# Cross-attention on one core: the first batch in another order, and T4 summed by accumulating DMAs

## The chip, the cores and the metric

The kernel runs on one core of a Trainium2 chip. The metric is the device time of one execution in microseconds; lower is better. Before the change the median of three runs is 695.43 us (695.27 to 696.22). Times inside the profile are microseconds from the first instruction of the profiled execution. PE is TensorE, DVE VectorE, ACT ScalarE, POOL GpSimd, SP SyncE; L12 is line 12 of the kernel.

## The reference

For each of 8 batches, with 512 channels and 1024 positions, all in float32:

```python
q = jnp.einsum('bcn,dc->bnd', x1, Wq) + bq              # d = 64
k = jnp.einsum('bcn,dc->bdn', x2, Wk) + bk[:, None]
v = jnp.einsum('bcn,dc->bdn', x2, Wv) + bv[:, None]
attn = jax.nn.softmax(jnp.einsum('bnd,bdm->bnm', q, k), axis=2)
return jnp.einsum('bcm,bnm->bcn', v, attn) + x1
```

## The kernel before

*Two products per batch.* The kernel never forms v. It first multiplies x2 by the attention weights (the y stage), then the result by Wv (the o stage), and adds bv and x1 at the end. Both products are cut into two by two blocks and done with Winograd's form of Strassen's algorithm: seven block products in place of eight, for sums of blocks that are formed beforehand. In the y stage the left blocks are `a["11"]` to `a["22"]` (x2, transposed by the host), the right ones `t["11"]` to `t["22"]`, which are the exponentials: `e[h]` holds the scores of one half h of the queries against all keys, 128 x 2 x 4 x 512, where the second axis is the half g of the keys and the third a tile i of 128 keys. So `t["11"]` and `t["21"]` are the two halves of `e[0]`, `t["12"]` and `t["22"]` those of `e[1]`.

The sums of the left blocks are S1 to S4 (`sum_a`, `left_sums`, L100), those of the right ones T1 to T4 (`sum_e`, `right_sums`, L258). Each is one operation of VectorE on 128 x 1024 elements, or for the T sums two, one for each pair of key tiles. `MULT` (L292) says which pair a product takes: product 1 takes 11 and 11, 2 takes 12 and 21, 6 takes S2 and T2, 7 takes S3 and T3, 5 takes S1 and T1, 3 takes S4 and 22, and 4 takes 22 and T4.

*A second level.* Products 3 and 4 of the y stage (and product 2 from batch 1 on) are cut once more in the same way: `inner_left` and `inner_right` form the inner sums (tiles aI and eI) on VectorE, `inner_product` (L362) multiplies them. `inner_right(s, 4, T4)` reads T4, and is its only reader. Within an inner product TensorE takes the inner products in the order 1, 7, 6, 2, 5, 4, 3: the first needs no sums, the second needs the inner S3 and T3, and T3 is the third of the four sums that `inner_right` forms.

*Softmax.* The scores of a tile are made by TensorE (`scores`) and copied to `e` by ScalarE. VectorE folds the tiles of a half into a maximum (`fold`, "max"), GpSimd takes it over the partitions (`highest`, a partition_all_reduce), VectorE subtracts it (`lower`, or `first_exponentials` for half 0 of the first batch), ScalarE takes the exponential. The denominators are sums of the same tiles: folds on VectorE (`sums`) or, for half 0 of the batches from 1 on, DMAs that add a tile onto another (`add_tile`); then `total` reduces them over the partitions on GpSimd and starts a small DMA into `few`; `shares` takes the reciprocal on VectorE and spreads it again by two DMAs (`row`, then `den`), the second waiting for the first.

*Order.* The kernel runs under a manual schedule: each engine executes its instructions in the order in which the code issues them, and waits by semaphores. `head` opens batch 0, `head_second` finishes its half 1, and `period` runs one batch and, woven in, the scores of the next. GpSimd's queue holds the column reductions and all accumulating and small DMAs; SP's holds the loads and stores. An instruction that waits holds back all that is behind it on its engine.

What matters of the order of VectorE in `period`: for batches from 1 on, T1 and T2 (`sum_e`), the sums of half 1, the evictions of product 2, T4 (`sum_t4`), S4, T3, then `inner_right` of product 4 (eI4), `inner_left` of product 3 (aI3), the maxima of the next batch's half 0, the four subtractions of that maximum, then `inner_right` of product 3 (eI3). In batch 0 the maxima come ahead of eI4 and the subtractions behind eI3. On GpSimd, for batches from 2 on: the shares of half 0 (`row`, `den`), the second denominator with its `few`, then the column maximum of the next batch. In batch 1 both denominators come first and the shares of half 0 behind them.

In `head`, VectorE forms S1 and S2 after it has handed the maximum of half 0 to GpSimd and before it subtracts the reduced maximum; TensorE makes three pairs of scores of half 1 (a pair is one tile of keys in both halves) ahead of product 1, and the fourth in `head_second`.

## Time and profile before

| what | value |
|---|---|
| median of the runs | 695.43 us (695.27 to 696.22) |
| the profiled execution's own time | 694.83 us |
| its span, first to last instruction | 693.0 us |
| TensorE busy | 685.8 us, 99% |
| VectorE busy | 604.5 us, 87% |
| ScalarE busy | 255.2 us, 37% |
| GpSimd busy | 186.9 us, 27% |
| queue of GpSimd's DMAs | 29.96 MB, 25.7% of 16 engines |
| granted TensorE clock | 1.000 |

A row of a timeline gives start, duration, engine, line, operation, the tile written and those read, the shapes, and how many instructions were merged; in brackets stands the idle time of the engine before it and what ended it. Names of tiles lose their numbers there: eT is any of T1, T2, T4, and eI the inner sums of any product. A DMA's row on GpSimd is its issue; when its data has landed stands in the list of issues, as a time from the issue. TensorE's matmuls are pipelined and their ends are modelled. Spans on GpSimd are rough.

### The profile page before, as it was taken

What the parts mean: (1) busy time and instruction counts of PE and PEld (TensorE: products, weight loads), DVE (VectorE), ACT (ScalarE), POOL (GpSimd) and SP (SyncE); (2) the same over time, 40 slices, a digit from 0 to 9 for tenths busy, and PEclk for the clock granted to TensorE, in tenths of its full rate; (3) what the DMA queues carried; (4) which work ended last, traced back from release to release, by engine and by line L of the source; (5) the groups of instructions that cost most, each with busy time, mean ns of one, the idle gap of its engine ahead of it and who ended that gap; (6) DMA issues with size and microseconds to landing.
All of it is one profiled execution on the core that took longest, in us unless ns stands there. A gap on an engine that the chain in (4) does not pass through costs nothing.

```text
span 693.0 us, 6395 instructions
## 1 busy us (share of the span) xinstructions
PE 685.8 (99%) x2188; PEld 353.4 (51%) x2188; DVE 604.5 (87%) x756; ACT 255.2 (37%) x402; POOL 186.9 (27%) x135
## 2 busy tenths in 40 slices
PE   8999999999999999999999999999999999999997
PEld 5333554535545355454654546454554545545563
DVE  1999999988999878998789987999689998999685
ACT  2733353145242543235432344413444235241120
POOL 0123113512322125222162222522223222423000
PEclk9999999999999999999999999999999999999999
DMA  9676256953567463865639457284742743369103
GB/s 307 254 233 226 58 183 129 260 157 76 183 128 210 149 116 142 166 183 151 107 138 191 157 166 181 67 190 140 183 78 55 172 136 60 77 115 251 31 1 121
DMA packets 42992, 102.72 MB, mean 148 GB/s; under 512 B 4688, under 2 KB 6992, under 8 KB 42960
## 3 DMA queue, kind: packets, MB, share of 16 engines
q1 hardware_dynamic: 25856, 70.13, 29.1%
q0 software_dynamic: 15696, 29.96, 25.7%
q10 hardware_dynamic: 1408, 2.23, 1.0%
q8 instruction: 17, 0.28, 0.2%
q14 instruction: 15, 0.12, 0.0%
HBM read 72.62 MB, written 16.81 MB: 129 GB/s over the span
## 4 chain that ended last, share of the span: by engine, by line
PE 95%; DMA 2%; ACT 1%; DVE 1%; SPq 1%; issue 0%; DVEq 0%
PE ps_ya L312 24%; PE ps_oa L312 16%; PE ps_i L362 14%; PE ps_oc L312 12%; PE ps_yc L312 9%; PE ps_s L190 6%; PE ps_k L148 4%; PE ps_q L148 4%; PE ps_yc L362 3%; PE ps_ya L362 3%; DMA a<-in_x2T_dram 1%; DMA x_head<-in_x_dram 1%; PE ps_sc L190 1%; PE ps_sa L190 1%; DVE aS L109 0%; ACT e L199 0%
## 5 line engine op out<-in xcount | busy, mean ns | idle before, releaser
L312 PE MATMUL ps_ya<-eT,aS 128*128 128x512 f32 x256 | 113.1, 596 | 0.0
L323 ACT COPY uy<-ps_ya 128x512 f32<-128x512 f32 x48 | 28.0, 587 | 163.8 <-PE ps_ya L312 158.0
L225 POOL PARTITION_ALL_REDUCE den<-sum x16 | 69.4, 4337 | 44.0 <-DVE sum L214 39.0
L248 DVE TENSOR_TENSOR e<-e,top 128x1024 f32<-128x1024 f32 x60 | 69.8, 1215 | 10.9 <-POOL top L220 10.9
L312 PEld LDWEIGHTS ps_ya<-eT,aS 128*128 128x128 f32 x256 | 48.0, 190 | 60.8 <-issue 59.7
L220 POOL PARTITION_ALL_REDUCE top<-max x16 | 31.3, 1957 | 162.4 <-DVE few L233 74.9
L252 ACT ACTIVATE e<-e 128x1024 f32<-128x1024 f32 x60 | 61.3, 1054 | 21.6 <-DVE e L248 20.1
L362 PE MATMUL ps_i<-eI,aI 128*128 128x256 f32 x276 | 66.0, 380 | 0.3 <-ACT e L199 0.3
L312 PE MATMUL ps_yc<-e,a 128*128 128x512 f32 x144 | 63.4, 593 | 0.0
L312 PE MATMUL ps_oa<-yT,w_S 128*128 128x512 f32 x128 | 57.6, 593 | 0.0
L312 PE MATMUL ps_oc<-y,w 128*128 128x512 f32 x128 | 57.5, 592 | 0.0
L312 PE MATMUL ps_ya<-e,a 128*128 128x512 f32 x128 | 56.3, 593 | 0.3 <-ACT e L243 0.3
L362 PEld LDWEIGHTS ps_i<-eI,aI 128*128 128x128 f32 x276 | 51.9, 190 | 8.2 <-ACT e L199 0.7
L199 ACT COPY e<-ps_s 128x1024 f32<-128x1024 f32 x46 | 45.7, 1028 | 19.1 <-PE ps_s L190 17.9
L323 ACT COPY uo<-ps_oa 128x512 f32<-128x512 f32 x48 | 27.9, 584 | 64.3 <-PE ps_oa L312 58.1
L190 PE MATMUL ps_s<-q,k 64*128 64x512 f32 x188 | 47.3, 608 | 0.8 <-ACT q L553 0.8
L261 DVE TENSOR_TENSOR eT<-e,eT 128x1024 f32<-128x1024 f32 x32 | 47.0, 1489 | 0.5
L312 PEld LDWEIGHTS ps_yc<-e,a 128*128 128x128 f32 x144 | 27.3, 190 | 34.8 <-issue 33.6
L521 POOL DMA_DIRECT2D sum<-e x21 | 25.7, 1224 | 69.5 <-DMA sum<-e 54.8
L371 ACT COPY d<-ps_i 128x256 f32<-128x256 f32 x64 | 22.3, 375 | 57.9 <-PE ps_i L362 57.9
L517 POOL DMA_DIRECT2D uo<-in_x_dram x21 | 25.0, 1191 | 68.9 <-DVE uo L514 63.1
L312 PEld LDWEIGHTS ps_ya<-e,a 128*128 128x128 f32 x128 | 24.3, 190 | 31.3 <-issue 29.6
(119 smaller groups left out, 1098.7 us busy)
## 6 DMA issues: line engine op xcount, KB each, us to landing
x_in_x_dram<-in_x_dram SPq DMA_DIRECT2D x60, 512.0 KB, 6.0
a<-in_x2T_dram SPq DMA_DIRECT2D x32, 512.0 KB, 7.0
sum<-e POOLq DMA_DIRECT2D x21, 512.0 KB, 5.1
uo<-in_x_dram POOLq DMA_DIRECT2D x21, 512.0 KB, 6.5
out_dram<-uo SPq DMA_DIRECT2D x21, 512.0 KB, 4.1
den<-row POOLq DMA_DIRECT2D x16, 256.0 KB, 3.5
r<-in_x_dram POOLq DMA_DIRECT2D x7, 512.0 KB, 5.9
out_dram<-r SPq DMA_DIRECT2D x7, 512.0 KB, 8.3
```

Of the source, the lines that this page charges most:

```text
L148: nc.tensor.matmul(ps[r, :], w_sb[:, c, :], s.x[:, c, ts(h, H)], start=(c == 0), stop=(c == CT - 1),)
L190: nc.tensor.matmul(ps[g], s.k[r, ts(i, P)], s.q[r, ts(h, H)], start=True, stop=True)
L199: nc.scalar.copy(e[:, :, i, :], whole)
L220: nc.gpsimd.partition_all_reduce(s.top[h], s.mx[h][:, 0, :], P, ReduceOp.max)
L225: nc.gpsimd.partition_all_reduce(s.den[h], s.mx[h][:, 0, :], P, ReduceOp.add)
L248: nc.vector.tensor_tensor(e, e, top, ALU.subtract)
L252: nc.scalar.activation(e, e, AF.Exp)
L261: nc.vector.tensor_tensor(t[k], t[x], t[y], ALU.subtract)
L312: nc.tensor.matmul(ps[:, n], left[ka][:, k, ts(j, P)], right[kb][:, k, n], start=opens and k == 0, stop=i in (2, 3, 4) and k == n_k - 1, s ...
L323: nc.scalar.copy(s.tmp[i][:, j, :], ps)
L362: nc.tensor.matmul(ps, s.inner[i][ka][:, k, :], s.inner[i, "t"][kb][:, k, :], start=opens and k == 0, stop=z in (2, 3, 4) and k == MH // 2 ...
L521: nc.gpsimd.dma_start(s.mx[h], s.e[h][:, :, i, :], accum_op=ALU.add)
```

## The change

Six things, of which the first concerns only the form of the second:

1. S2 becomes 11 - S1 where it was S1 - 11, and T2 becomes T1 - 22 where it was 22 - T1. S4 and T4 add S2 and T2 where they subtracted them. Both factors of product 6 change sign, so it stays; S4 and T4 stay as they were. The same holds for the inner sums and for the o stage.
2. `sum_t4` no longer uses VectorE: ScalarE copies the block 21 into T4 in two halves, and two DMAs on GpSimd's queue add the halves of T2 to it. `sum_t4` stands in `period` and is called once for every batch.
3. In `head`, S1 and S2 are formed behind the subtractions of half 0.
4. The third pair of scores of half 1 is made behind product 1, in `head_second`, and its copies with it.
5. The fold of tile 1 into the sum of half 0 comes after the fold of tile 1 into the maximum of half 1.
6. The folds of tiles 2 and 3 into the sum of half 0 come in `period` behind T1 and T2, for batch 0 alone.

```diff
@@ left_sums, and the same in LEFT
-                "S2": ("S1", "11", ALU.subtract),
+                "S2": ("11", "S1", ALU.subtract),
...
-                "S4": ("12", "S2", ALU.subtract),
+                "S4": ("12", "S2", ALU.add),
@@ right_sums, and the same in RIGHT
-        x, y = {"T1": ("12", "11"), "T2": ("22", "T1"), "T3": ("22", "12"), "T4": ("21", "T2")}[k]
-        nc.vector.tensor_tensor(t[k], t[x], t[y], ALU.subtract)
+        x, y = {"T1": ("12", "11"), "T2": ("T1", "22"), "T3": ("22", "12"), "T4": ("21", "T2")}[k]
+        nc.vector.tensor_tensor(t[k], t[x], t[y], ALU.add if k == "T4" else ALU.subtract)
@@ sum_t4
-        s.t["T4"] = sb.tile([P, MH, H], F32, tag="eT4", name=f"eT4_{s.b}")
-        sum_e(s, "T4")
+        s.t["T4"] = t4 = sb.tile([P, MH, H], F32, tag="eT4", name=f"eT4_{s.b}")
+        for i in (0, 2):
+            nc.scalar.copy(t4[:, i : i + 2, :], s.t["21"][:, i : i + 2, :])
+        for i in (0, 2):
+            nc.gpsimd.dma_start(t4[:, i : i + 2, :], s.t["T2"][:, i : i + 2, :], accum_op=ALU.add)
@@ head
         highest(s, 0, halves=False)
-        sum_a(s, "S1", "S2")
         more_queries(*tiles[1:])
         load_x(states[1], x1)
-        copies = [scores(s, 1, 0), scores(s, 1, 1), scores(s, 1, 2, "c")]
+        copies = [scores(s, 1, i) for i in range(2)]
         for g in range(2):
             for i in range(MH):
                 first_exponentials(s, g, i)
         for copy in copies:
             copy()
+        sum_a(s, "S1", "S2")
+        fold(s, 1, 1, "max", ALU.max)
         fold(s, 0, 1, "sum", ALU.add)
-        fold(s, 0, 2, "sum", ALU.add)
-        fold(s, 1, 1, "max", ALU.max)
-        fold(s, 0, 3, "sum", ALU.add)
@@ head_second
-        scores(s, 1, 3)()
+        copies = [scores(s, 1, 2, "c"), scores(s, 1, 3)]
+        for copy in copies:
+            copy()
@@ period
         sum_e(s, "T1", "T2")
+        if s.b == 0:
+            for i in range(2, MH):
+                fold(s, 0, i, "sum", ALU.add)
         if s.b < 2:
             total(s, 0)
```

More of the change, by code (lines that the diff above doesn't have):

```diff
@@ L326 @@
         ("S1", "21", "22", ALU.add),
-        ("S2", "S1", "11", ALU.subtract),
+        ("S2", "11", "S1", ALU.subtract),
         ("S3", "11", "21", ALU.subtract),
-        ("S4", "12", "S2", ALU.subtract),
+        ("S4", "12", "S2", ALU.add),
     )
@@ L332 @@
         ("T1", "12", "11", ALU.subtract),
-        ("T2", "22", "T1", ALU.subtract),
+        ("T2", "T1", "22", ALU.subtract),
         ("T3", "22", "12", ALU.subtract),
-        ("T4", "21", "T2", ALU.subtract),
+        ("T4", "21", "T2", ALU.add),
     )
```

## The prediction

> **What bounds the kernel now.** I read the page's busy shares and its chain first, then the list of what TensorE waited for, then the timelines of VectorE, GpSimd and TensorE around the products that read T4, and last the landing times of accumulating DMAs.

> ```profile
> PE 685.8 (99%) x2188; PEld 353.4 (51%) x2188; DVE 604.5 (87%) x756; ACT 255.2 (37%) x402; POOL 186.9 (27%) x135
> PE 95%; DMA 2%; ACT 1%; DVE 1%; SPq 1%; issue 0%; DVEq 0%
> ```
> ```profile
> PE ps_warm L598 <- DVE warm L595: 1.0, 1, 1.0
> PE ps_q L549 <- DMA x_head<-in_x_dram: 1.0, 1, 1.0
> PE ps_s L190 <- ACT q L553: 0.8, 1, 0.8
> PE ps_ya L312 <- ACT e L243: 0.3, 1, 0.3
> PE ps_i L362 <- ACT e L199: 0.3, 1, 0.3
> ```
> TensorE is the bound, and its waits sum to 3.4 us; after 25 us it waits once, 0.29 us at 590 us. So work taken from VectorE gains next to nothing, and whatever makes TensorE wait is paid in full. The question is how much slack each step has, and T4 has the least to spare: here is batch 1, from VectorE, GpSimd and TensorE in turn.

> ```profile
> 138.15 2.33 DVE L261 TENSOR_TENSOR eT<-e,eT 128x1024 f32<-128x1024 f32 x2
> 143.80 0.68 DVE L355 TENSOR_TENSOR eI<-eT 128x512 f32<-128x512 f32 x1
> 154.30 4.63 DVE L248 TENSOR_TENSOR e<-e,top 128x1024 f32<-128x1024 f32 x4 [1.82 <-POOL top L220]
> 160.18 0.69 DVE L355 TENSOR_TENSOR eI<-e 128x512 f32<-128x512 f32 x1
> ```
> ```profile
> 137.76 0.59 POOL L227 DMA_DIRECT2D few<-den  x1 [0.30 <-POOL den L225]
> 141.00 0.54 POOL L237 DMA_DIRECT2D den<-row  x1 [1.93 <-DMA row<-few]
> 152.49 1.78 POOL L220 PARTITION_ALL_REDUCE top<-max  x1 [10.95 <-DVE few L233]
> ```
> ```profile
> 160.27 1.03 PE L362 MATMUL ps_i<-e,aS 128*128 128x256 f32 x4
> 161.14 1.89 PE L362 MATMUL ps_i<-eI,aI 128*128 128x256 f32 x8
> ```
> L261 at 138.15 is T4. L355 at 143.80 opens eI4, the right sums of product 4, and reads T4. Behind it VectorE does, without a gap, aI3, the maxima of the next batch, their column maximum on GpSimd (the one idle of 1.82), four subtractions, and eI3, whose third sum T3 runs 160.18 to 160.87. TensorE reads that T3 at 161.14: slack 0.27 us.

> **The change, part by part.** The definition of T4 is shared, so all eight batches get the copies and the DMAs, not the first alone.

> *Signs.* S2, S4, T2, T4 keep their shapes and counts: nothing.

> *T4 on its engines.* VectorE loses two operations of 2.33 to 2.34 us together per batch (4.64 beside a reduction). ScalarE gains two copies of 128x1024, 1.03 each by L529, 2.1 per batch; in batches 1 to 6 they fall into the 4.79 us it idles before the copies of product 6, in batch 7 into 5.83, in batch 0 between 48.4 and 51.3: hidden, with 0.8 us left in batch 0. GpSimd gains two DMA issues of about 1.2 us. In batches 1 to 7 they stand between the denominators and the column maximum, where GpSimd idles 7.0 to 13.4 us; in batch 0 they stand ahead of the second denominator, after the first one's issue. SP's queue is not touched.

> *When T4 lands.* The profile has no T4 DMA; the nearest rows are the 21 sums that add an SBUF tile to an SBUF tile, also 512 KB, and one place where two accumulating DMAs are issued back to back:

> ```profile
> sum<-e POOLq DMA_DIRECT2D x21, 512.0 KB, 5.1
> ```
> ```profile
> 108.74 1.19 POOL L517 DMA_DIRECT2D uo<-in_x_dram  x1 [9.04 <-DVE uo L514]
> 109.49 1.66 POOL L521 DMA_DIRECT2D sum<-e  x1
> ```
> ```profile
> uo<-in_x_dram POOLq DMA_DIRECT2D x1, 512.0 KB, 5.7
> sum<-e POOLq DMA_DIRECT2D x1, 512.0 KB, 7.4
> ```
> The first landed 5.7 us after its issue, the second 7.4 after its own: at 116.9, 2.5 us behind the first and 8.15 us after the first issue. T4's two start from a source like the sums (5.1), so I take 7.9 us from the first issue to both landed. Ends: 7.45 (fastest sum 5.0, plus 2.45) and 9.5 (the pair issued at 117.22 and 117.94, queued behind a third, was in at 126.7). I go by the rows, because they are accumulating DMAs on the same queue.

> [...]

> *What VectorE then waits for.* eI4 needs both halves. Without T4, VectorE is there 2.3 us sooner than before, and the DMAs are later than that in every batch from 1 on. Delay of eI4 = landing minus its old start; all up to eI3 follows it, the 1.82 us wait for the maximum too, as that reduction stands behind eI4. Stall of TensorE = old end of T3 in eI3 + delay + 0.1 (the exponential at 24.29 took 0.60, TensorE began at 24.97) minus the time at which TensorE read it. From the timelines (us):

> | batch | first T4 issue | both in | old eI4 start | delay | old T3 end | TensorE reads | stall |
> |---|---|---|---|---|---|---|---|
> | 1 | 141.57 | 149.9 | 143.80 | 6.1 | 160.87 | 161.14 | 5.9 |
> | 2 | 221.62 | 229.5 | 225.31 | 4.2 | 242.36 | 245.60 | 1.1 |
> | 3 | 305.05 | 313.0 | 309.73 | 3.2 | 326.79 | 330.06 | 0.1 |
> | 4 | 389.76 | 397.7 | 394.44 | 3.2 | 411.49 | 414.52 | 0.3 |
> | 5 | 474.30 | 482.2 | 477.99 | 4.2 | 495.05 | 498.98 | 0.4 |
> | 6 | 558.82 | 566.7 | 562.50 | 4.2 | 579.56 | 579.86 | 4.0 |
> | 7 | 639.70 | 647.6 | 642.25 | 5.4 | 648.37 | 653.88 | 0 |

> The issue is 0.57 after GpSimd's last earlier DMA (few of half 1; in batch 1 den<-row at 141.00, whose 256 KB, in at 144.5, I give 0.4 us in front of T4). Batch 6 has little slack because TensorE has no queries to project there; batch 1 because its aI4 comes later and GpSimd does the first shares late. Sum: 11.8 us. Each batch's GpSimd chain is started by TensorE's results, so a stall in one batch shifts the next as a whole and is not given back. What comes behind eI3 on VectorE is covered: it idled 2.8 to 4.2 us before L431 in batches 1 to 5, and in batch 6, where only 1.4, L431 waits for the stalled TensorE. The exponentials behind the subtractions end late on ScalarE too: its copy of the first inner bank then comes about 0.4 us after TensorE restarts, inside the 0.86 us of the product in between.

> *Batch 0.* T4 is issued near 56 and in at about 64.5; eI4 stands at 68.79: hidden, by 4 us. *The opening:*

> ```profile
> 20.45 1.22 DVE L109 TENSOR_TENSOR aS<-a,a 128x1024 f32<-128x1024 f32 x1
> 21.71 1.94 DVE L109 TENSOR_TENSOR aS<-aS,a 128x1024 f32<-128x1024 f32 x1
> 23.57 4.89 DVE L242 TENSOR_TENSOR e<-e,top 128x512 f32<-128x512 f32 x8
> ```
> S1, S2 leave this place; the reduction that runs beside them (20.63, 2.68 us) takes 1.77 where VectorE only waits (318.43). Then the subtractions begin at 22.44 instead of 23.57, and product 1 at 23.84 instead of 24.97: minus 1.13. But the third pair of scores, 0.86 us that TensorE did in this gap, now stands behind product 1: net minus 0.27. If the reduction stays at 2.68, minus 0.2 plus 0.86, so plus 0.66. S1 and S2 go behind the subtractions, 27.3 to 29.7, where VectorE next waits for a copy that ends near 29.9. The maximum of half 1 is then asked for at 36.4 (36.62), and T2's second half is done near 48.75, 0.3 us before product 6 reads it. The two late sums (2.4 us) fill the place of T4 (2.35), so eI3 of batch 0 stays near 76.13 to 76.5 against TensorE at 76.3: plus 0 to 0.2, taken as 0.1. Opening and batch 0: minus 0.2.

> *Sum.* 11.8 - 0.2 = plus 11.6 on the profiled execution: span 693.0 to 704.6, its time 694.83 to 706.4. The median of the runs, 695.43, stands 0.6 above that execution: 707.0. At the ends of the landing the stalls come to 9.7 us (7.45) and 22.9 us (9.5), with the opening 704.9 and 719.

> **The rivals.** *Not slower: T4 lands before VectorE asks.* Decisive are batches 1 and 6: slack 0.2 us, so T4 would have to be in 2.4 us (by 144.0) and 3.9 us (by 562.7) after its first issue. Then only the opening counts: 695.2. For it: VectorE loses 2.3 us of work per batch. Against it: it then only waits sooner, and of the 21 sums none landed under 5.0.

> *Slower by less: the halves move side by side.* If the second half lands 6.8 us or less after the first issue (1.7 behind the first), batches 2 to 5 are free, and 1 and 6 give 4.8 and 2.9: 703.0; if both are in after 5.1, 3.1 and 1.2, so 699.5. Against it: the 2.5 us between the two landings at 114.4 and 116.9.

> *Slower by more: the queue is fuller.* At 9.5 us each batch from 2 to 5 pays 1.7 to 2.7 and batch 7 some 1.5: 718. For it: the sums range up to 7.4. Against it: in batch 3 the loads issued at 299.16 are the last on the other queue until 315.47, so T4 moves nearly alone.

> **How the numbers follow.** Forecast 0.76; side by side 0.10; fuller queue 0.10; not slower 0.04. The forecast holds 704.9 to about 711 (landing up to 8.5). Taking in most of the second and a good part of the third gives 702 to 714. A measurement of this kernel tells about 0.2% (1.4 us) from no change; beyond that on the fast side nothing in the rows could carry it: the opening has 1.1 us to give. Faster 0.01, same 0.03, slower 0.96.

> **What would show it.** TensorE's waits list inner products (L366) on VectorE's eI: about 5 to 6 us at batch 1 and 4 at batch 6, the longest. VectorE idles 4 to 8 us before eI4 (L359), released by the DMA eT<-eT. T4's pair lands 7.5 to 8.5 us after its first issue. Product 1 opens near 23.9. It is wrong if eI4 waits for nothing, if T4 lands in under 6 us, or if the longest new wait stands elsewhere, such as at batch 0's T2.

## The result and the profile after

The changed kernel takes 718.11 us (median of 5 runs, 715.97 to 726.01) against 695.43 us: ratio 1.0337, 95% interval 1.0309 to 1.0365. The profiled execution took 716.75 us with a span of 715.0, so the span grew by 22.0 us where the prediction had 11.6. The direction, the wait and its places came as predicted; the sum had no term for TensorE's clock, priced the stalls too short, and came to about half. The range ended at 714 and did not hold the time.

Busy shares, the clock row and the chain from the page of the changed kernel:

```profile
PE 692.5 (97%) x2188; PEld 356.4 (50%) x2188; DVE 585.3 (82%) x740; ACT 272.2 (38%) x418; POOL 200.7 (28%) x151
...
PEclk9999999998999999999999999999999998999999
...
PE 21%; DMA 2%; DVE 2%; issue 1%; ACT 1%; POOL 1%; DVEq 0%; ACTq 0%; POOLq 0%
```

VectorE does 19.2 us less than before, ScalarE 17.0 and GpSimd 13.8 more. TensorE runs the same 2188 matmuls, but its busy time is 6.7 us higher, and two digits of the clock row are an 8. That is the first sign of a loss that is not a wait. The chain here is followed back only to 506 us and its shares are not those of the whole span.

What TensorE waited for (total, times, longest):

```profile
PE ps_i L366 <- ACT sum L533: 15.6, 5, 6.4
PE ps_warm L602 <- DVE warm L599: 1.0, 1, 1.0
PE ps_s L190 <- ACT q L557: 0.8, 1, 0.8
PE ps_q L553 <- DMA x_head<-in_x_dram: 0.7, 1, 0.7
```

One new wait, at inner product 7 of product 3 as predicted. The row names ScalarE's first copy of the next sum, because that ended last, 0.05 us ahead; what inner product 7 waits for in the program is VectorE's third sum in eI3. In batch 1 that sum ends at 167.90 and TensorE goes on at 168.05. The same 0.15 us lie between the two in batch 0 of the run with T4 on VectorE below, where ScalarE makes no such copy and the row names VectorE. Batch 1 from VectorE, GpSimd and TensorE, then the stalls of the other batches:

```profile
150.82 0.69 DVE L359 TENSOR_TENSOR eI<-eT 128x512 f32<-128x512 f32 x1 [8.85 <-DMA eT<-eT]
...
161.34 4.63 DVE L248 TENSOR_TENSOR e<-e,top 128x1024 f32<-128x1024 f32 x4 [1.83 <-POOL top L220]
...
167.22 0.68 DVE L359 TENSOR_TENSOR eI<-e 128x512 f32<-128x512 f32 x1
```
```profile
141.64 0.54 POOL L237 DMA_DIRECT2D den<-row  x1 [2.21 <-DMA row<-few]
142.16 1.79 POOL L276 DMA_DIRECT2D eT<-eT  x2
```
```profile
160.62 1.03 PE L366 MATMUL ps_i<-e,aS 128*128 128x256 f32 x4
168.05 3.75 PE L366 MATMUL ps_i<-eI,aI 128*128 128x256 f32 x8 [6.40 <-ACT sum L533]
...
257.34 1.97 PE L366 MATMUL ps_i<-eI,aI 128*128 128x256 f32 x8 [1.84 <-ACT sum L533]
342.97 1.97 PE L366 MATMUL ps_i<-eI,aI 128*128 128x256 f32 x8 [0.93 <-ACT sum L533]
513.42 1.97 PE L366 MATMUL ps_i<-eI,aI 128*128 128x256 f32 x8 [1.29 <-ACT sum L533]
599.67 3.75 PE L366 MATMUL ps_i<-eI,aI 128*128 128x256 f32 x8 [5.13 <-ACT sum L533]
```

T4 is asked for at 142.16, and at 150.82 VectorE, idle for 8.85 us, starts eI4. Here and below a pair of DMAs counts as in, or landed, when VectorE starts on it; the record of the landing itself lies some 0.1 us earlier (150.69). The reader should also compare the second number of the five rows: the same eight matmuls, inner products 7 and 6, take 1.97 us in three batches and 3.75 us behind the two long stalls. The view by stretches, cut into four pieces of 3.41 us, shows why (after the length: busy time and count of TensorE, its weight loads, VectorE, ScalarE, GpSimd; then the granted clock, the DMA share and GB/s):

```profile
163.36:166.78 3.42, 0.00 (x0) 0.00 (x0) 3.39 (x5) 3.18 (x4) 0.56 (x1) 1.00 0.27 77
166.78:170.19 3.41, 2.14 (x5) 1.81 (x6) 2.93 (x5) 1.55 (x4) 1.23 (x1) 0.50 0.04 7
170.19:173.60 3.41, 3.41 (x9) 2.69 (x9) 0.00 (x0) 0.69 (x2) 0.00 (x1) 0.50 0.86 147
173.60:177.02 3.42, 3.42 (x16) 2.44 (x17) 1.71 (x3) 0.65 (x2) 1.21 (x1) 1.00 0.54 93
```

After a stretch in which TensorE did nothing, its clock is 0.50 for two such stretches, 6.83 us, and TensorE does 9 matmuls in the time of 16 or so. Two halved stretches come once more, from 596.86 us, there behind a stretch in which TensorE idled for 2.32 of 3.41 us.

With this the 22.0 us can be added up. "Stall" is the start of inner product 7, less the start of inner product 1 of the same product, less the 0.87 us between them without a wait; "half clock" is half of the time that TensorE worked at 0.50; "lateness" is the start of product 3 after the change less that before, which shows the term of the batch above.

| batch | lateness at product 3 | stall | half clock |
|---|---|---|---|
| 1 | 0.35 | 6.56 | 2.8 |
| 2 | 9.73 | 2.00 | 0 |
| 3 | 11.81 | 1.09 | 0 |
| 4 | 12.98 | 0 | 0 |
| 5 | 12.99 | 1.44 | 0 |
| 6 | 14.51 | 5.29 | 2.0 |
| end | 22.0 | | |

0.35 + 16.4 + 4.8 = 21.5; the other 0.5 us is spread.

### The profile page after: what moved, and what is told of

The parts are those of the page before. It is cut to its first block, busy times and chain, and to the rows that moved or that the text cites. A ratio compares the mean times of both kernels' runs of the same rounds, so it can differ in the third digit from the quotient of the medians.

```text
span 715.0 us, 6445 instructions
## 1 busy us (share of the span) xinstructions
PE 692.5 (97%) x2188; PEld 356.4 (50%) x2188; DVE 585.3 (82%) x740; ACT 272.2 (38%) x418; POOL 200.7 (28%) x151
## 5 line engine op out<-in xcount | busy, mean ns | idle before, releaser
L366 PE MATMUL ps_i<-eI,aI 128*128 128x256 f32 x276 | 70.1, 396 | 15.9 <-ACT sum L533 15.6
L225 POOL PARTITION_ALL_REDUCE den<-sum x16 | 68.9, 4308 | 42.5 <-DVE sum L214 42.3
L220 POOL PARTITION_ALL_REDUCE top<-max x16 | 30.6, 1915 | 173.0 <-DVE few L233 88.4
L248 DVE TENSOR_TENSOR e<-e,top 128x1024 f32<-128x1024 f32 x60 | 69.8, 1217 | 11.0 <-POOL top L220 11.0
L366 PEld LDWEIGHTS ps_i<-eI,aI 128*128 128x128 f32 x276 | 53.9, 199 | 26.3 <-ACT sum L533 17.5
L199 ACT COPY e<-ps_s 128x1024 f32<-128x1024 f32 x46 | 45.7, 1028 | 18.9 <-PE ps_s L190 18.4
L327 ACT COPY uo<-ps_oa 128x512 f32<-128x512 f32 x48 | 28.0, 585 | 64.5 <-PE ps_oa L316 57.2
L359 DVE TENSOR_TENSOR eI<-eT 128x512 f32<-128x512 f32 x16 | 11.0, 688 | 49.1 <-DMA eT<-eT 49.1
L190 PE MATMUL ps_s<-q,k 64*128 64x512 f32 x188 | 47.2, 607 | 0.8 <-ACT q L557 0.8
L316 PEld LDWEIGHTS ps_yc<-e,a 128*128 128x128 f32 x144 | 27.3, 190 | 34.8 <-issue 33.6
L521 POOL DMA_DIRECT2D uo<-in_x_dram x21 | 25.1, 1195 | 67.6 <-DVE uo L518 67.6
L210 DVE TENSOR_TENSOR max<-max,e 128x1024 f32<-128x1024 f32 x30 | 36.8, 1226 | 4.4 <-ACT e L197 1.0
## 6 DMA issues: line engine op xcount, KB each, us to landing
x_in_x_dram<-in_x_dram SPq DMA_DIRECT2D x60, 512.0 KB, 6.8
a<-in_x2T_dram SPq DMA_DIRECT2D x32, 512.0 KB, 6.5
sum<-e POOLq DMA_DIRECT2D x21, 512.0 KB, 5.3
uo<-in_x_dram POOLq DMA_DIRECT2D x21, 512.0 KB, 6.4
out_dram<-uo SPq DMA_DIRECT2D x21, 512.0 KB, 4.7
eT<-eT POOLq DMA_DIRECT2D x16, 512.0 KB, 6.1
r<-in_x_dram POOLq DMA_DIRECT2D x7, 512.0 KB, 7.3
```

Source lines behind the costliest of these rows:

```text
L190: nc.tensor.matmul(ps[g], s.k[r, ts(i, P)], s.q[r, ts(h, H)], start=True, stop=True)
L199: nc.scalar.copy(e[:, :, i, :], whole)
L210: nc.vector.tensor_tensor(f, e[:, :, 0, :] if i == 1 else f, e[:, :, i, :], op)
L220: nc.gpsimd.partition_all_reduce(s.top[h], s.mx[h][:, 0, :], P, ReduceOp.max)
L225: nc.gpsimd.partition_all_reduce(s.den[h], s.mx[h][:, 0, :], P, ReduceOp.add)
L248: nc.vector.tensor_tensor(e, e, top, ALU.subtract)
```

## The experiments

Theory A: the whole loss is TensorE waiting because VectorE waits for T4's DMAs ahead of eI4, plus the halved clock behind the longest of these stalls. Rivals: B, the new opening has a part in it; C, the copies and the added DMA traffic slow other things; D, the halved clock has another cause than idle time of TensorE. Two more come later, on what sets the landing of an early T4: F, the loads that move at the same time, and G, the reduction that GpSimd runs beside it. Where lines of T4's code are added or left out, line numbers differ by a few.

**T4 on VectorE, opening as changed.**

```diff
-            nc.scalar.copy(t4[:, i : i + 2, :], s.t["21"][:, i : i + 2, :])
-        for i in (0, 2):
-            nc.gpsimd.dma_start(t4[...], s.t["T2"][...], accum_op=ALU.add)
+        sum_e(s, "T4")
```

> The changed kernel with T4 computed on VectorE again in all batches (no copies, no accumulating DMAs); signs and opening stay as changed. Theory A (the whole loss is TensorE waiting because VectorE waits for T4's DMAs, plus the halved clock behind the two longest of these stalls): inner product 7 waits in no batch, granted clock 1.000, time 695.0 to 696.3. In the changed kernel's trace TensorE reaches product 3 of batch 1 0.35 us later than before (160.62 against 160.27), so near 695.8. Theory B (the new opening has a part in the loss): 698 or more.

Measured: 697.86 us, 1.0037 (1.0024 to 1.0049), clock 0.999 to 1.000. Most of the loss is gone, but not all: 2.4 us stay, where theory A had at most 0.9; theory B's sign, 698 or more, is missed by 0.1. The trace puts most of them in batch 0, 2.2 us in two waits of TensorE:

```profile
57.70 1.13 PE L190 MATMUL ps_s<-q,k 64*128 64x512 f32 x4 [0.58 <-ACT e L199]
78.83 1.96 PE L362 MATMUL ps_i<-eI,aI 128*128 128x256 f32 x8 [1.62 <-DVE eI L355]
```

The two sums that the change moved to batch 0 (2.4 us on VectorE) have no room there unless T4 leaves VectorE in that batch, just as the prediction's batch 0 step had it. So the opening is not free by itself; it is paid by batch 0's T4.

**T4 by copies and DMAs in batch 0 alone.**

```diff
+        if s.b > 0:
+            sum_e(s, "T4")
+            return
         for i in (0, 2):
             nc.scalar.copy(...)
```

> The changed kernel with T4 by copies and DMAs in batch 0 alone, on VectorE in the others: signs and opening as changed. The kernel with T4 on VectorE everywhere (697.9) lost 1.6 us at eI3 of batch 0, behind the two sums that came there; with T4 off VectorE in that batch this stall goes. Theory A: no wait of TensorE above 0.3 us after 25 us, clock 1.000, 694.9 to 695.7, the same as with eI4 behind eI3 (695.1). Theory B (the opening costs something by itself): 697 or more.

Measured: 695.58 us, 1.0003 (0.9994 to 1.0012). After 25 us TensorE waits nowhere for more than 0.3 us. With the run above it shows that batch 0's DMAs are worth 2.3 us to the new opening (697.86 to 695.58), and that opening and batch 0 together come to no change. Theory B falls: what costs 22 us is T4 in batches 1 to 7.

**T4 alone, opening as before.** The kernel before, with the signs and the new `sum_t4`.

> The kernel before with the signs and the copies and accumulating DMAs for T4 alone; the opening stays as before. Theory A: the same stalls of inner product 7 as in the changed kernel (about 6.5, 2, 1, 0, 1.5, 5 us in batches 1 to 6), granted clock 0.98 to 0.99, 715 to 720. Theory B: below 712, by as much as the opening costs.

Measured: 717.3 us, 1.0309 (1.0265 to 1.0353), runs 713.01 to 721.11. Stalls in the profiled run:

```profile
168.70 3.75 PE L366 MATMUL ps_i<-eI,aI 128*128 128x256 f32 x8 [7.62 <-ACT sum L533]
258.32 1.97 PE L366 MATMUL ps_i<-eI,aI 128*128 128x256 f32 x8 [2.02 <-ACT sum L533]
344.25 1.97 PE L366 MATMUL ps_i<-eI,aI 128*128 128x256 f32 x8 [1.23 <-ACT sum L533]
514.15 1.97 PE L366 MATMUL ps_i<-eI,aI 128*128 128x256 f32 x8 [0.73 <-ACT sum L533]
600.66 3.75 PE L366 MATMUL ps_i<-eI,aI 128*128 128x256 f32 x8 [5.39 <-ACT sum L533]
```

Same places, same sizes within 1.2 us, the same loss. This is theory A again.

**eI4 behind eI3.** Copies, DMAs and traffic stay; only the order on VectorE differs.

```diff
         if s.b:
-            inner_right(s, 4, s.t["T4"], "eT2")
             inner_left(s, 3, s.a["S4"], "aI3")
...
         if s.b:
             inner_right(s, 3, s.t["22"], "eT1")
+            inner_right(s, 4, s.t["T4"], "eT2")
```

> The changed kernel with the right sums of product 4 (eI4, the reader of T4) moved behind the right sums of product 3 (eI3) in batches 1 to 7. Copies, accumulating DMAs and their traffic all stay; only nothing of eI3 is queued behind the wait for T4 any more. Theory A: no stall of inner product 7, clock 1.000, 694.8 to 696.3; eI4 waits for no DMA, as T4 lands some 8 us before VectorE gets to it. Theory C (the copies on ScalarE and the 8 MB more on the GpSimd queue slow other things by themselves): 700 or more, with waits at other places.

Measured: 695.13 us, 0.9995 (0.9986 to 1.0003). What TensorE waited for in this kernel is short:

```profile
PE ps_warm L602 <- DVE warm L599: 1.0, 1, 1.0
PE ps_s L190 <- ACT q L557: 0.8, 1, 0.8
PE ps_q L553 <- DMA x_head<-in_x_dram: 0.6, 1, 0.6
PE ps_i L366 <- ACT e L199: 0.3, 1, 0.3
```

All 16 copies and 16 DMAs are there and cost nothing: theory C falls. The 23 us are not the price of the DMAs but of what was queued behind their wait on VectorE. This version beats the changed kernel by 23 us and cannot be told from the kernel before: VectorE has some 14 us less to do (590.9 busy, before 604.5), and since TensorE is busy 99% of the span in both, that buys nothing.

**T4 on VectorE in batches 1 and 6 alone.** `if s.b in (1, 6): sum_e(s, "T4"); return` ahead of the copies.

> The changed kernel with T4 on VectorE in batches 1 and 6 alone, the two with the long stalls. Theory A: the stalls of batches 2, 3 and 5 stay at 2.0, 1.1 and 1.4 us, none of them halves the clock (1.000), and the time is 695.8 plus 4.5: 699 to 701.5. Theory D (the halved clock comes from something other than the length of the stall): clock below 1.000 still, 702 or more.

Measured: 702.56 us (700.63 to 705.86), 1.0107 (1.0081 to 1.0132), 1 us over the expectation's end. The remaining stalls were 1.93, 2.10 and 1.23 us, as expected in batches 2 and 5 and 1 us longer in batch 3; and the clock, which theory A had at 1.000, fell once, behind that stall:

```profile
334.46:337.88 3.42, 1.32 (x7) 0.87 (x6) 3.35 (x7) 2.62 (x4) 0.69 (x1) 1.00 0.19 62
337.88:341.29 3.41, 3.41 (x10) 2.65 (x9) 2.17 (x5) 0.74 (x2) 0.54 (x1) 0.50 0.76 131
341.29:344.70 3.41, 3.41 (x17) 2.58 (x17) 1.56 (x3) 0.65 (x2) 1.20 (x1) 1.00 0.20 35
```

A stall of only 2.10 us, over at 336.94, was followed by 3.41 us at 0.50 from 337.88. So a stall as long as those of batches 1 and 6 (6.40 and 5.13 us) is not needed: theory A in the form written down, with a halved clock behind the longest stalls alone, is too simple. Both signs that the expectation gave for theory D came, a clock below 1.000 and 702 us or more. What is left to test is whether idle time of TensorE is the cause at all. In this profiled run TensorE also came to the scores behind product 6 of batch 0 1.6 us later than in the changed kernel (56.55 against 54.99), which may be part of the 3.0 us by which it is longer than the next of the four.

**VectorE made late without any DMA.** The kernel before, the first sum of eI4 repeated.

```diff
-            nc.vector.tensor_tensor(v[k], v[x], v[y], op)
+            for _ in range(REPEAT[s.b] if i == 4 and z == 0 else 1):
+                nc.vector.tensor_tensor(v[k], v[x], v[y], op)
+    REPEAT = (1, 4, 11, 12, 13, 15, 5, 1)
```

> The kernel before (T4 on VectorE, no new DMA), with the first sum of eI4 done over again 3, 10, 11, 12, 14 and 4 times more in batches 1 to 6, at 0.6 us each: VectorE comes late to eI3 by 1.8, 6.1, 6.7, 7.3, 8.5 and 2.4 us. Theory A (lateness of VectorE before eI3 is all there is to it): less the slack of each batch (0.1, 3.1, 3.1, 2.9, 3.8, 0.15 with 0.15 us for the signal) inner product 7 stalls about 1.7, 3.0, 3.6, 4.4, 4.7 and 2.3 us, 19.7 in all, and behind the stalls over about 3 us the clock is halved for one or two windows of 3.4 us, each costing up to 1.7 to 3.4 us: 695.4 + 19.7 + 6 to 13 = 721 to 728. Theory D (the halving belongs to the DMAs): the same stalls, clock 1.000, about 715.

Measured: 735.92 us, 1.0592 (1.0572 to 1.0612). A repeat took 0.72 us (four in 2.86), not 0.6, so VectorE was late by 2.2 to 10 us and the waits came to 26.4 us instead of 19.7. The time lies beyond theory A's 721 to 728 and far from theory D's 715:

```profile
163.50 1.97 PE L365 MATMUL ps_i<-eI,aI 128*128 128x256 f32 x8 [2.29 <-ACT sum L532]
252.20 3.75 PE L365 MATMUL ps_i<-eI,aI 128*128 128x256 f32 x8 [4.01 <-ACT sum L532]
343.88 3.75 PE L365 MATMUL ps_i<-eI,aI 128*128 128x256 f32 x8 [4.35 <-ACT sum L532]
437.02 3.75 PE L365 MATMUL ps_i<-eI,aI 128*128 128x256 f32 x8 [5.58 <-ACT sum L532]
531.45 3.75 PE L365 MATMUL ps_i<-eI,aI 128*128 128x256 f32 x8 [7.35 <-ACT sum L532]
```

Batch 6 had 2.85. The clock was halved behind five of the six, not behind the 2.29 us, for 34 us in all (its mean is 0.976); the expectation's "over about 3 us" was an estimate, as the 2.85 us halved it too. Half of TensorE's work in that time is 12.7 us. Counted as in the table above, with the 0.15 us from VectorE's sum to TensorE, the stalls are 27.4 us, and 694.8 + 27.4 + 12.7 = 734.9 against 735.1 for this execution. Lateness alone makes the stalls and the halved clock; the DMAs are only one way to be late.

**Idle matmuls in the two long stalls.**

```diff
...
             inner_product(s, i, z, ps, opens, *copies)
+            if i == 3 and z == 1 and s.b in (1, 6):
+                for _ in range(10 if s.b == 1 else 8):
+                    nc.tensor.matmul(third_bank[:, 1, left], w["11"][:, 0, 0:P], w["12"][:, 0, :], start=True, stop=True)
```

> The changed kernel with idle matmuls (128x256, their result is read by nobody) on TensorE between inner products 1 and 7 of product 3: 10 in batch 1 and 8 in batch 6, at 0.43 us each 4.3 and 3.4 us, less than the stalls there (6.5 and 5.3 us). VectorE and the landing of T4 stay as they are, so inner product 7 begins when it did; only TensorE's idle time is filled. Theory A (the clock is halved because TensorE stood idle): no halved stretch behind these two stalls, the x8 row of inner product 7 takes 1.97 instead of 3.75 us there, and the time falls by 4.8 us to about 712 (711 to 714). Theory D (the halving comes from something else in these places, or costs nothing because it lies beside waits): clock 0.990 as before and 716 to 718.

Measured: the profiled execution 712.27 us with clock 1.000, as theory A has it (711 to 714); inner products 7 and 6 of batch 1 take 1.99 us behind the filled stall:

```profile
161.40 4.48 PE L436 MATMUL ps_i<-w,w 128*128 128x256 f32 x20
167.60 1.99 PE L366 MATMUL ps_i<-eI,aI 128*128 128x256 f32 x8 [1.72 <-DVE eI L359]
```

The median is 715.78 (ratio 1.0281, 1.0258 to 1.0303), between theory A's 711 to 714 and theory D's 716 to 718: the other three runs have mean clocks of 0.995 to 0.998. They have no trace; that stalls of about 2 us in other batches halved the clock there, as in the run above, is likely but not shown. With TensorE kept at work, the two halvings did not come in this execution, while each of the 13 waits of 2.33 to 7.62 us in the table at the end, from traces with and without T4's DMAs, brought one. So theory D falls.

**T4 issued earlier.** In batches 2 to 7, `sum_t4(s)` ahead of `sums(s, 1)`.

> The changed kernel with T4's copies and DMAs asked for ahead of the second sum of the denominators in batches 2 to 7: on GpSimd the two issues then stand right behind den<-row of half 0, ahead of the reduction and the issue for half 1, some 4.2 us earlier; batch 1 keeps its order. If the place of the issue is what makes T4 late, and the landing takes 7.3 to 8.8 us as before: eI4 waits 2.5 to 4 us instead of 5 to 7.5, the stalls of batches 2, 3 and 5 (2.0, 1.1, 1.4) are gone, batch 6 stalls 1.3 instead of 5.3 with no halved clock behind it, batch 1 keeps 6.5 and its halved clock; the time falls by 10 to 11 us to about 706 (704 to 709). If T4 is instead late through what else moves at that time, the landing gets longer by as much and the time stays above 712.

Measured: 718.98 us, 1.0346 (1.0319 to 1.0372). This missed the 706 us by 13; what came is the other case of the expectation, a longer landing and more than 712 us. Counted back from product 3 on TensorE, T4 was issued 4.5 us earlier in batch 2 and 5.0 in batch 6, and it landed 0.6 us later and 0.3 us earlier; batch 6, GpSimd and VectorE:

```profile
571.13 0.57 POOL L237 DMA_DIRECT2D den<-row  x1 [6.40 <-DMA row<-few]
571.69 1.82 POOL L276 DMA_DIRECT2D eT<-eT  x2
573.14 3.84 POOL L225 PARTITION_ALL_REDUCE den<-sum  x1
```
```profile
583.99 0.69 DVE L359 TENSOR_TENSOR eI<-eT 128x512 f32<-128x512 f32 x1 [6.93 <-DMA eT<-eT]
```

12.3 us from first issue to landing, where the changed kernel had 574.88 to 582.44, 7.56. In batches 2 to 7 it took 10.9 to 13.0. The wait of batch 6 fell from 5.13 to 4.86 us, that of batch 2 rose from 1.84 to 2.42, and the first two matmuls behind it took 1.05 us (two take 0.59 at full clock, at 345.64 in the changed kernel). So something else holds T4 back; two runs ask what.

**The loads of a21 and a22 moved away from T4**, alone and together with the early issue.

```diff
-        if n:
+        if n and s.b == 0:
             load_a(n, "21", "22")
...
             scores_and(n, 0, "c", next_queries if nn else nothing)
+            if s.b and nn:
+                load_a(n, "21", "22")
...
             load_a(n, "12")
+            if s.b and not nn:
+                load_a(n, "21", "22")
```

> The changed kernel with the loads of a21 and a22 (1 MB, put on SP's queue with a11 just ahead of T4) moved behind the next batch's loads of x in batches 1 to 5, and behind the load of a12 in batch 6; T4 is issued where it was. With T4 issued early it landed 11 to 13 us after its first issue instead of 7.3 to 8.8, at nearly the same moment. Theory F (the DMA engines are full there: T4 lands when the loads ahead of it and its own 1 MB have gone through): in the changed kernel only the first 2 us of T4 lie beside these loads, so the landing falls from 7.5 to 8.8 to about 7.3 us, where it stood in batch 4, the stalls by 0.3 to 1.4 us each, 2 to 4 us in all, and the time to about 713 to 716. Theory G (T4 is slowed by the reduction that GpSimd runs beside it when it is issued early, not by loads): landing and time as in the changed kernel, 716 to 719.

> Both: T4's copies and DMAs asked for ahead of the second sum of the denominators in batches 2 to 7, and the loads of a21 and a22 moved away from it. Theory F (full DMA engines): T4 lands some 7.3 us after its first issue instead of 11 to 13, so 3 to 4 us sooner than in the changed kernel; no stall in batches 2 to 5, 1.3 to 2 us in batch 6, batch 1 as before with its halved clock: 704 to 708. Theory G (the reduction beside it on GpSimd): landing stays 10 us or more, 714 or more.

Measured: alone 711.42 us, 1.0221 (1.0186 to 1.0256); with the early issue 707.66, 1.0157 (1.0127 to 1.0187). From first issue to both halves in (us):

| batch | as changed | loads later | early issue | early issue, loads later |
|---|---|---|---|---|
| 2 | 7.89 | 7.22 | 12.95 | 9.63 |
| 5 | 7.33 | 7.34 | 11.63 | 8.56 |
| 6 | 7.56 | 7.16 | 12.30 | 9.46 |

Batches 3 and 4 are left out, since VectorE was not released by the DMA there in the last column; with the loads later alone batch 3 fell from 8.75 to 7.18. Without the loads the late T4 of batches 2 to 6 lands in 7.2 to 7.3 us, and the time falls by 6.7 us in the median and 4.6 in the profiled executions, more than the 2 to 4 expected: batch 6 waits 3.86 instead of 5.13 us and the eight matmuls behind that take 2.75 instead of 3.75, batch 1 waits 5.40 instead of 6.40. Not all of this is the landing: counted back from product 3, T4 was issued 0.5 us earlier in batch 1 and 0.9 in batch 6, since GpSimd's wait for row<-few was that much shorter; why is not shown. With the early issue the loads account for about 3 us of the landing, and the time is 11.3 us better than with the early issue alone and within F's expectation. Batch 7 is a control: the four loads of x that lie beside an early T4 there were moved in neither kernel, and it took 12.7 us with the early issue and 14.2 with both changes. From first issue to both halves in, batch 6 with the early issue, with both changes and with the loads later alone (the DMA share stands next to last):

```profile
571.69:583.99 12.30, 12.30 (x37) 5.18 (x36) 5.37 (x3) 5.55 (x8) 5.87 (x5) 1.00 0.96 241
563.74:573.20 9.46, 9.46 (x30) 3.74 (x28) 5.11 (x3) 3.75 (x7) 5.61 (x5) 1.00 0.93 222
570.37:577.53 7.16, 7.16 (x25) 2.81 (x24) 1.51 (x3) 4.41 (x6) 1.81 (x3) 1.00 0.78 147
```

The engines are 96% busy in the first. So the loads that share the DMA engines hold T4 back, theory F. But 8.6 to 9.6 us are not 7.3: the load of a11 and an output still lie beside an early T4, den<-row (256 KB on the same queue) stands 0.6 us ahead of it and not 4.6, and the reduction runs on GpSimd. The engines are 93% busy there too, which speaks for the transfers; G's part in the rest was not tried by itself.

## Why the prediction was wrong

**Right.** All batches got the DMAs; TensorE's inner product 7 waits for eI3 behind eI4 behind T4; batches 1 and 6 are the longest, 4 and 7 stall not at all; the releaser of eI4 is the DMA eT<-eT; ScalarE's copies cost nothing. The eT<-eT pair landed in 7.26 to 8.75 us, in the mean of batches 1 to 7 7.85, against 7.9 taken. That the mean agrees so well is partly luck: in three runs with the same code for T4 in these batches (T4 alone, the one without batches 1 and 6, the idle matmuls), pairs took 7.15 to 11.1 us. The opening: the reduction beside idle VectorE took 1.78 (1.77 said), product 1 opened at 24.07, which is 23.84 and the 0.22 us by which the first load was later. T4 of batch 0 was hidden, and batch 0's place for the two sums is shown by the run with T4 on VectorE. Opening and batch 0 came to plus 0.35 instead of minus 0.2, 0.2 of it that load. Of the 10.4 us by which the sum fell short, 4.8 are the clock, 4.6 the stalls, 0.5 this, and 0.5 are not placed.

**Wrong: the sum had no term for the clock.** "Sum: 11.8 us" priced a stall by its length alone. Two stalls also cost 4.8 us behind them, at half clock; the idle matmuls, the repeats and the 2.10 us stall show the cause. The trace of before could not show it, as TensorE never idled longer than 1.04 us at a time there. Behind the 2.10 us stall the clock was at 0.50 for 3.41 us, behind the 6.40 and 5.13 us ones for 6.83 us each.

**Wrong in size: the table of stalls**, 16.4 instead of 11.8 us. Its formula holds; two columns were off. "First T4 issue" was taken at the old distance from TensorE, and "both in" as a constant 7.9 (8.33 in batch 1). With what was measured (issue: distance of the first issue to product 3 on TensorE, before less after):

| batch | predicted stall | issue later by | landing longer by | sum | measured |
|---|---|---|---|---|---|
| 1 | 5.9 | 0.24 | 0.33 | 6.47 | 6.56 |
| 2 | 1.1 | 0.87 | 0 | 1.97 | 2.00 |
| 3 | 0.1 | 0.13 | 0.85 | 1.08 | 1.09 |
| 4 | 0.3 | -0.16 | -0.64 | under 0 | 0 |
| 5 | 0.4 | 1.57 | -0.57 | 1.40 | 1.44 |
| 6 | 4.0 | 1.55 | -0.34 | 5.21 | 5.29 |

The constant came from one pair, 8.15 us; another pair of that profile, issued as closely at 616.64 and 617.36, was in after 9.4 us, near the 9.5 kept for the slow end. In sum over the batches the issue is the larger part. The step said "The issue is 0.57 after GpSimd's last earlier DMA" and placed that DMA by the trace of before. But ahead of it stands GpSimd's wait for row<-few, 2 KB that the DMA ahead of it writes to DRAM. It waited 5.67, 5.75 and 5.80 us in batches 2, 5 and 6 before, and 6.39, 6.83 and 7.36 after:

```profile
570.25 0.57 POOL L237 DMA_DIRECT2D den<-row  x1 [7.36 <-DMA row<-few]
570.85 3.18 POOL L225 PARTITION_ALL_REDUCE den<-sum  x1
574.33 0.55 POOL L227 DMA_DIRECT2D few<-den  x1 [0.29 <-POOL den L225]
574.88 1.81 POOL L276 DMA_DIRECT2D eT<-eT  x2
```

That is all of batch 6's 1.55 us (7.36 less 5.80) and 0.72 of batch 2's 0.87; in batch 5 it is 1.08 of 1.57, and the reduction behind it takes 0.5 longer. This wait varies: 6.79, 5.69, 7.10, 5.52 and 6.04 us for half 0 of batches 2 to 6 in the run with repeats, which has no T4 DMA. Why it grew where it did stays open.

**The rivals.** Landing before VectorE asks (0.04), and the halves side by side, which needed 6.8 us or less, did not come: no pair of the changed kernel landed under 7.2 us. The fuller queue, 718 us, gave the right time for mostly the wrong reason: it priced a landing of 9.5 us in every batch, while of batches 1 to 7 only 1 and 3 took more than 8 (8.66 and 8.75); the other part was issue and clock. Where it was right is that other transfers matter: the loads of a21 and a22. It was argued against with the other queue being idle after 299 us in batch 3, but those loads, issued 5 us ahead of T4 (311.93 to 316.99 us), were still moving when it came (issue to landing 7.0 us in the median), and batch 3 had the longest landing, 8.75.

## What to carry to other kernels

Work given to a DMA cost nothing in itself here (695.13 us, ratio 0.9995, with all 16 copies and 16 DMAs); what costs is the first thing in the queue of the waiting engine that has an early reader, so the reader of a slow result goes behind the work that others wait for (715.0 to 693.2 us of span by moving four sums). A stall of TensorE is to be priced with its clock: behind 6.40, 5.13 and 2.10 us it cost another 2.8, 2.0 and 1.7 us here, behind 2.29 us nothing. Issuing T4 5.0 us earlier brought its landing in batch 6 forward by 0.3 us, with the DMA engines 96% busy meanwhile; look at which loads were issued just ahead.

## What the hardware showed

| wait (us) | run | batch | matmuls behind it (us) |
|---|---|---|---|
| 7.62 | T4 alone | 1 | 3.75 |
| 7.35 | VectorE made late | 5 | 3.75 |
| 6.40 | the changed kernel | 1 | 3.75 |
| 6.29 | T4 issued earlier | 1 | 2.04 (four) |
| 5.58 | VectorE made late | 4 | 3.75 |
| 5.39 | T4 alone | 6 | 3.75 |
| 5.13 | the changed kernel | 6 | 3.75 |
| 4.86 | T4 issued earlier | 6 | 3.37 |
| 4.35 | VectorE made late | 3 | 3.75 |
| 4.01 | VectorE made late | 2 | 3.75 |
| 3.86 | loads later | 6 | 2.75 |
| 2.42 | T4 issued earlier | 2 | 1.05 (two) |
| 2.33 | T4 issued earlier, loads later | 6 | 3.07 |
| 2.29 | VectorE made late | 1 | 1.97 |
| 2.10 | T4 on VectorE in batches 1 and 6 | 3 | 2.83 |
| 2.02 | T4 alone | 2 | 1.97 |
| 1.93 | T4 on VectorE in batches 1 and 6 | 2 | 1.97 |
| 1.84 | the changed kernel | 2 | 1.97 |

Behind the 13 waits of 2.33 us and more these matmuls were slowed, behind the three of 2.02 us and less they were not; in between 2.10 us slowed them and 2.29 us did not. What decides there is not shown. The clock cost 1.7 us behind the 2.10 us (half of the 3.41 us at 0.50).

The times of the changed kernel spread widely (715.97 to 726.01 us at mean clocks of 0.983 to 0.990; 694.89 to 695.61 us at 0.999 to 1.000 for the kernel with eI4 behind eI3, which has no such wait). The 726.01 us run has no trace, and what made it longer than the others is not shown.

Two accumulating DMAs of 512 KB, issued one behind the other, were in 7.16 to 7.34 us after the first issue with the loads later (batches 2, 5 and 6; DMA share 0.78 in batch 6), 7.26 to 8.75 us in the changed kernel, and 10.9 to 13.0 us with the early issue (share 0.96 in batch 6).
